# One product for three k chunks, weight sums moved, last products at fixed places and a second queue for the first loads, in a two-layer cross-attention kernel

## The chip, the cores and the metric

The kernel runs on one core of a Trainium2 chip. The metric is the device time of one execution in microseconds (us), launch to end. Several executions are timed and the median is given; one more execution is recorded by the hardware profiler, and all durations of single instructions come from that one.

## The reference

Two layers of cross-attention with a residual work on `x` (8 batches, 100 queries, 640 channels) and a context of 722 tokens of 1024 channels. The first 77 tokens are "text", the other 645 are "ip". Each layer has its own weights; all are f32. Shortened:

```python
q = split_heads(x @ Wq)                     # 20 heads of 32 channels
k, v       = text @ Wk, text @ Wv
k_ip, v_ip = ip @ Wk_ip, ip @ Wv_ip
out_text = softmax(q @ k.T * scale) @ v
# layer 0
out_ip = softmax(q @ k_ip.T * scale) @ v_ip
# layer 1: a shared term is added to the ip scores, and a mask is multiplied in
text_probs = softmax(q_all_heads @ k_all_heads.T * scale)
sem = (text_probs @ text) @ ip.T * scale
out_ip = (softmax(q @ k_ip.T * scale + 0.5 * sem) * mask) @ v_ip
x = (out_text + out_ip) @ Wo + bias + x
```

The context is the same in both layers, so the keys and values of both layers can be made without waiting for the attention.

## The kernel before

**Units and visits.** A unit `u` is one layer of one batch: 16 units, 0 to 7 for layer 0. Units go in `PAIRS` of two. The channels are cut into five chunks `c` of 128 (four heads). One step of the attention, called a visit here, is one pair (u, c) of the list `ORDER`: 80 visits, about 20 us each.

**The attention of a visit.** `scores` (L989) multiplies q by k into PSUM in two parts (512 and 210 columns). DVE takes maxima, ACT the exponentials (L1012, L1044), DVE the factors (L1034 to L1052). In the visit after, `transposes` (L1080) turn the probabilities by TensorE in six steps, through two PSUM tiles `pspt`; DVE or ACT copies each one out (L1087, L1085). Then `values` (L1103) multiplies by v into `pv`. `out_piece` (L901, `pso`) and `q_piece` apply the output weights and the next layer's q; the residual is added by DVE at L906. These small products take their PSUM from the same two tiles as `pspt`. `sem_text`, `sem_logits`, `sem_transpose` and `sem_scores` make the shared term of layer 1.

**Making k and v.** The 645 ip tokens of a pair are cut into five blocks of 128 (the last has 133). `pair_tasks` lists the products for the blocks (0, 1), (2, 3) and (4). Each matrix product is made of 2 x 2 halves by a scheme with seven products instead of eight: `seven` returns the seven steps in the order first, sixth, second, seventh, fifth, fourth, third. The steps use quarters of the weights (`b11` to `b22`) and sums of them (`t1` to `t4`, made by `weight_sums`, L134 to L137, in place where it can be), and in the same way sums of the tokens (`token_sums`, `third_sum`, `fourth_sum`). The sums for the pair that follows are made before it begins (`first_sums`). PSUM results `psv_*` and `psk_*` go through two banks; DVE and ACT move them to a tile of the pool `made` (two buffers), and GpSimd stores that to `k_d` and `v_d` in device memory. SP loads k and v back for each visit.

`v_steps` makes v (L613). `k_steps` makes the first four k chunks (L641). The fifth chunk of both layers is made together, only in layer 0's pairs, by `k4_steps` (L674) from weights of its own in `W4`, which lie in tiles that layer 1 uses later (`kt5`, `gt`, `g`, `sem`). For the block 4, `k_steps([0, 1])` multiplies matmuls of 133 columns, two chunks side by side (266 columns of a PSUM bank of 512), and `k4_steps` one chunk (133).

**The last pair.** Units 14 and 15 are made by `two_chunks` (L788, L793; v and k of two chunks in one product), and v of the fifth chunk by `fifth_chunk` (L828, `psv`, two halves for each of five blocks).

**What sets the order.** On TensorE, DVE and ACT the order is that of the code; on SP and GpSimd it is set by a scheduler of the framework. `production` gives every step a time in visits: `spread` puts a list of steps between two times so that each visit gets an even share, by the estimated cost of each step (the first number of a task; a cost of 0.0 marks work that is no product). `between` then puts the steps that are due into four slots of a visit: before the first transposes, between pairs of them, and before and after the last pair; from visit 74 on the third slot lies behind the last transposes. `apart` brings in the step that follows, when it is due within 0.4 visits (0.1 from visit 76 on), so that two parts of the attention don't stand side by side. `insert` puts extra tasks a number of steps ahead of a mark; `("k 4", 1, ...)` means ahead of the last step of block 4's k.

**The beginning.** The first lines of the work load, by SP alone, `xt` and `wq` in five row blocks each. The first product (`psq`, L279) needs one of each.

Of the kernel before, what the change touches and what calls it, by code (L numbers as in the profile page):

```python
# [44 lines left out]
def two_layer_xattn(  # L45
# [200 lines left out]
    with ExitStack() as es:  # L246
# [4 lines left out]
        )  # L251
        wq0 = []
        for k in range(NC_):
            nc.sync.dma_start(xt[:, :2, k], x_t[:, :2, k])
            t = fp.tile([P, C], F32, tag="wr", name=f"wq0_{k}", bufs=NCC)
            nc.sync.dma_start(t, wq[0][k * P : (k + 1) * P, :])
            wq0.append(t)
        for g in range(1, B // 2):
            nc.sync.dma_start(xt[:, 2 * g : 2 * g + 2], x_t[:, 2 * g : 2 * g + 2])
# [8 lines left out]
        nc.sync.dma_start(left_sb, left_t)  # L268
        nc.sync.dma_start(bias_sb, bias.rearrange("l p c -> p l c"))
        nc.sync.dma_start(mask_sb[:, 1:2], mask)  # L270


        for g in range(B // 2):
# [273 lines left out]
    def pair_tasks(us):  # L547
# [15 lines left out]
        for js in ((0, 1), (2, 3), (4,)):  # L563
# [68 lines left out]
            def k_steps(rs, js=js, n=n, operands=operands, pos=pos):  # L632

                made, ko = {}, {}
                m = n * len(js)

                def product(ps, which, go_on):
                    tokens = operands(which, None if len(js) == 2 else js[0])
                    for i, r in enumerate(rs):
                        for k in range(HK):  # L640
                            nc.tensor.matmul(  # L641
                                ps[:, i * m : (i + 1) * m],
                                lhsT=W["k", WHICH[which]][:, k, r * P : (r + 1) * P], rhs=tokens(k),
                                start=(i == 0 and k == 0 and not go_on), stop=(k == HK - 1), skip_group_check=True,
                            )

                def step(i):
                    if i == 0:
                        o = ko[0] = opool.tile([P, 2, 2, len(rs), m], F32, tag="made", name=f"ko_{us[0]}_{js[0]}_{rs[0]}")
                        made[0] = seven(  # L650
                            f"psk_{us[0]}_{js[0]}_{rs[0]}", product,
                            tuple(o[:, h, m].rearrange("p r n -> p (r n)") for h in range(2) for m in range(2)),
                        )
                    made[0][i]()
                    if i < 6:
                        return
                    for h, u in enumerate(us):
                        for j in js:
                            p0 = pos[j] * n
                            dst = k_d[u][:, :4, BLOCKS[j][0] : BLOCKS[j][1]].rearrange("p (m r) n -> p m r n", r=2)  # L660
                            for i, r in enumerate(rs):
                                nc.gpsimd.dma_start(dst[:, :, r], ko[0][:, h, :, i, p0 : p0 + n])  # L662

                return [(1.8, lambda i=i: step(i)) for i in range(7)]

            def k4_steps(js=js, n=n, operands=operands, pos=pos):

                made, ko = {}, {}
                m = n * len(js)

                def product(ps, which, go_on):
                    tokens = operands(which, None if len(js) == 2 else js[0])
                    for k in range(HK):
                        nc.tensor.matmul(  # L674
                            ps[:, :m], lhsT=W4[WHICH[which]][:, k, :], rhs=tokens(k),
                            start=(k == 0 and not go_on), stop=(k == HK - 1), skip_group_check=True,
                        )

                def step(i):
                    if i == 0:  # L680
                        o = ko[0] = opool.tile([P, 2, 2, m], F32, tag="made", name=f"k4_{us[0]}_{js[0]}")
                        made[0] = seven(
                            f"psk4_{us[0]}_{js[0]}", product, tuple(o[:, h, l2] for h in range(2) for l2 in range(2))
                        )
                    made[0][i]()
                    if i < 6:
                        return
                    for h, u in enumerate(us):
                        for l2 in range(2):
                            for j in js:  # L690
                                nc.gpsimd.dma_start(
                                    k_d[u + B * l2][:, 4, BLOCKS[j][0] : BLOCKS[j][1]],
                                    ko[0][:, h, l2, pos[j] * n : (pos[j] + 1) * n],
                                )

                return [(1.75 if len(js) == 2 else 0.95, lambda i=i: step(i)) for i in range(7)]

            def head(j, begin=begin):

                return [(0.0, lambda: begin(j))]  # L700
# [7 lines left out]
            first = us[0] == 0 and js[0] == 0  # L708
            if first:
                tasks.append((0.0, lambda: [load(j) for j in range(3)]))  # L710
            ks_ = k_steps([0]) + k_steps([1]) if len(js) == 2 else k_steps([0, 1])
            if first:

                v_load = (0.0, lambda: load_wv(wvi[0]))
                v_sums = (0.0, lambda: (weight_sums("v", HC, (nc.vector, nc.gpsimd)), load_text(us)))
                v = v_steps(0)
                tasks += head(0) + head(1) + [(0.0, load_w4), v_load] + with_sums(0, with_sums(1, ks_[:7]))
                tasks += [v_sums] + ks_[7:] + [(0.0, w4_sums)] + k4_steps()
                tasks += v[:2] + [(0.0, text_sum)] + v[2:] + v_steps(1)
            else:  # L720

# [4 lines left out]
                for j in js:  # L726
# [385 lines left out]
    def production():  # L1112
# [88 lines left out]
    def small_work(n):  # L1201
# [200 lines left out]
```

## Time and profile before

| | |
|---|---|
| median of 3 executions | 2058.15 us (2058.02 to 2060.34) |
| the profiled execution's own time | 2060.31 us |
| its span, first to last instruction | 2058.5 us |
| mean granted clock of TensorE | 0.999 |
| DMA, mean over the span | 123 GB/s |

The span is what the rows of the profile divide among the engines; the time of an execution also has a little around it. The profiled execution is one of the longer ones of these four. A row of instructions names the line, the engine, the operation, what is written and read, and the shapes. f32 matmuls show as two records each. PE is TensorE, PEld its weight loads, DVE is VectorE, ACT is ScalarE, POOL is GpSimd, SP issues loads. A few matmul records in a hundred can be missing.

The page in 40 slices of the span (tenths of busy time):

```text
PE   8999999999999999999999999999999999999998
DVE  2211222246555455554556665655665667788777
ACT  1001000033433333333333344444444545566666
```

The first fifth of the span has no attention yet: it makes the text's k and v and the first pair. The new layer's value products begin at about 1107 us, and the last ten visits take up the stretch from about 1917 us.

### The profile page before, as it was taken

How to read it: one execution, taken by the hardware profiler on the slowest of the kernel's cores; microseconds unless marked ns; L12 is line 12 of the kernel's file. 1: busy time of each engine (PE TensorE's matmuls, PEld its weight loads, DVE VectorE, ACT ScalarE, POOL GpSimd, SP SyncE). 2: the span in 40 equal slices, each digit the busy share in tenths (PEclk: the TensorE clock that was granted, in tenths of full speed). 3: DMA queues.
4: the chain of work that ended last, by engine and by line, in shares of the span. 5: the costliest groups of instructions: out<-in, count | busy, mean ns of one | idle time of the engine just before them, and what ended most of it. 6: DMA issues, size and time to landing. Idle time of an engine off the chain costs nothing. (4 is left out here: it accounts for less than half of the span.)

```text
span 2058.5 us, 38749 instructions
## 1 busy us (share of the span) xinstructions
PE 2028.2 (99%) x15154; PEld 1568.4 (76%) x15154; DVE 1118.0 (54%) x3053; ACT 785.0 (38%) x2255; POOL 310.2 (15%) x445
## 2 busy tenths in 40 slices
PE   8999999999999999999999999999999999999998
PEld 8676767776777867778677777777777778888876
DVE  2211222246555455554556665655665667788777
ACT  1001000033433343333333344444544445566666
POOL 3212312111111101111111001001010101111110
PEclk9999999999999999999999999999999999999999
DMA  9545223323432534326255354336342536545461
GB/s 330 155 131 170 88 75 92 98 76 93 115 94 74 155 96 107 85 89 171 71 146 141 102 156 121 84 99 179 100 117 79 152 95 168 165 125 151 120 180 54
DMA packets 296340, 252.20 MB, mean 123 GB/s; under 512 B 46622, under 2 KB 265170, under 8 KB 296158
## 3 DMA queue, kind: packets, MB, share of 16 engines
q1 hardware_dynamic: 274382, 181.29, 32.6%
q0 software_dynamic: 21776, 68.44, 9.4%
q8 instruction: 119, 1.95, 0.4%
q14 instruction: 63, 0.52, 0.1%
HBM read 180.74 MB, written 68.93 MB: 121 GB/s over the span
## 5 line engine op out<-in xcount | busy, mean ns | idle before, releaser
L1012 ACT ACTIVATE p<-sc,st 100x512 f32<-100x512 f32 (+1 forms) x320 | 165.5, 529 | 217.6 <-DVE st L998 135.4
L1087 DVE COPY pt<-pspt 128x400 f32<-128x400 f32 (+1 forms) x319 | 175.5, 568 | 102.5 <-PE pspt L1080 93.3
L1044 ACT ACTIVATE p<-p,st 100x512 f32<-100x512 f32 x320 | 207.6, 713 | 56.0 <-DVE st L1038 55.8
L1080 PEld LDWEIGHTS pspt<-ident,p 100*128 100x128 f32 (+1 forms) x1920 | 187.7, 137 | 44.3 <-DVE res L906 6.2
L1080 PE MATMUL pspt<-ident,p 100*128 100x100 f32 (+1 forms) x1920 | 211.9, 250 | 8.2 <-DVE res L906 3.8
L1012 ACT ACTIVATE p<-p,st 100x512 f32<-100x512 f32 (+1 forms) x320 | 176.7, 554 | 81.8 <-DVE st L1004 81.7
L1085 ACT COPY pt<-pspt 128x400 f32<-128x400 f32 x161 | 79.2, 492 | 287.5 <-PE pspt L1080 287.1
L613 PE MATMUL psv_a<-wv,x 128*128 128x397 f32 (+1 forms) x560 | 185.8, 474 | 0.4
L662 POOL DMA_DIRECT2D k_d<-ko x140 | 100.0, 718 | 506.1 <-DVE ko L223 455.1
L613 PE MATMUL psv_d<-wv,s 128*128 128x320 f32 (+1 forms) x560 | 174.3, 454 | 0.0
L613 PEld LDWEIGHTS psv_a<-wv,x 128*128 128x128 f32 x560 | 103.0, 189 | 68.8 <-issue 12.6
L1004 DVE CUSTOM_DVE_ANT_0 p<-sc,sem 100x512 f32<-100x512 f32 (+1 forms) x320 | 138.7, 490 | 21.7 <-PE sc L989 21.5
L613 PEld LDWEIGHTS psv_d<-wv,s 128*128 128x128 f32 x560 | 104.1, 190 | 54.8 <-issue 4.3
L998 DVE TENSOR_REDUCE st<-sc 100x2 f32<-100x1024 f32 (+1 forms) x160 | 125.2, 824 | 29.0 <-PE sc L989 29.0
L989 PE MATMUL sc<-k,q 32*100 32x210 f32 (+1 forms) x1280 | 138.5, 502 | 0.9 <-DMA k<-k_d 0.9
L641 PE MATMUL psk_d<-s,wk 128*128 128x256 f32 (+1 forms) x672 | 136.5, 348 | 0.0
L628 POOL DMA_DIRECT2D v_d<-vo x70 | 38.8, 555 | 647.2 <-DVE gst L603 327.2
L641 PE MATMUL psk_a<-x,wk 128*128 128x256 f32 (+1 forms) x672 | 135.7, 347 | 0.6 <-ACT ko L197 0.6
L641 PEld LDWEIGHTS psk_a<-x,wk 128*128 128x128 f32 x672 | 109.0, 189 | 21.4 <-issue 5.0
L641 PEld LDWEIGHTS psk_d<-s,wk 128*128 128x128 f32 x672 | 108.2, 189 | 18.5 <-issue 4.8
L613 PE MATMUL psv_e<-wvt,x 128*128 128x397 f32 (+1 forms) x280 | 92.6, 472 | 0.0
L1103 PEld LDWEIGHTS pv<-pt,v 128*32 128x32 f32 x3200 | 67.5, 110 | 26.8 <-issue 13.6
(225 smaller groups left out, 3325.0 us busy)
## 6 DMA issues: line engine op xcount, KB each, us to landing
x<-ip_t SPq DMA_DIRECT2D x80, 512.0 KB
k<-k_d SPq DMA_DIRECT2D x80, 322.5 KB
v<-v_d SPq DMA_DIRECT2D x80, 320.0 KB
v_d<-vo POOLq DMA_DIRECT2D x70, 320.0 KB, 2.7
k_d<-ko POOLq DMA_DIRECT2D x112, 128.0 KB, 4.8
o<-wo SPq DMA_DIRECT2D x35, 320.0 KB
x<-ip_t SPq DMA_DIRECT2D x20, 532.0 KB
q<-wq SPq DMA_DIRECT2D x20, 320.0 KB
```

What stands on the lines that cost most here:

```text
L613: nc.tensor.matmul(ps[:, :m], lhsT=tokens(k)[:, :P], rhs=w[:, k, :], start=(k == 0 and not go_on), stop=(k == HK - 1), skip_group_check=True,)
L641: nc.tensor.matmul(ps[:, i * m : (i + 1) * m], lhsT=W["k", WHICH[which]][:, k, r * P : (r + 1) * P], rhs=tokens(k), start=(i == 0 and k == ...
L662: nc.gpsimd.dma_start(dst[:, :, r], ko[0][:, h, :, i, p0 : p0 + n])
L989: nc.tensor.matmul(scs[i // 2][:S, i % 2, : k1 - k0], lhsT=qs_[u][rows, c, :], rhs=ks[u, c][rows, k0:k1], start=True, stop=True)
L998: nc.vector.tensor_reduce(st[:, part, 2 * h : 2 * h + 2], scs[h][:S, :, :n], AX.X, ALU.max, negate=True)
L1004: nc.vector.tensor_tensor_reduce(out=p[:, i, k0 : k0 + n], in0=scs[h][:S, i % 2, :n], in1=sems[u][:, k0 : k0 + n], scale=-1.0, scalar=3.0e ...
L1012: nc.scalar.activation(dst, dst if l else scs[h][:S, i % 2, :n], AF.Exp, bias=st[:, part, i : i + 1], scale=-1.0 if l else 1.0, accum_out= ...
L1044: nc.scalar.activation(p[:, i, :KA], p[:, i, :KA], AF.Copy, scale=mul[:, 0, i : i + 1])
L1080: nc.tensor.transpose(ps[:rows, i * S : (i + 1) * S], pr[u, c][:, i, j * P : j * P + rows], ident[:S, :S])
L1085: nc.scalar.copy(dst, src)
L1087: nc.vector.tensor_copy(dst, src)
L1103: nc.tensor.matmul(ps[32 * i : 32 * i + 32, :S], lhsT=lhs, rhs=pt[:rows, j, i * S : (i + 1) * S], start=(j == 0), stop=(j == 5),)
```

## The change

It has four parts.

1. `k_steps` takes the chunk index 2 for the fifth chunk, with the weights of `W4`; `k4_steps` is gone. For two blocks at a time the fifth chunk stays a set of products of its own, with an estimated cost of 1.8 in place of 1.75. For block 4 in layer 0 all three chunks are side by side in one set of seven products (399 columns), with an estimated cost of 2.7 where there were 0.95 and 1.8.
2. At the change of layers (pair 3), the first two of layer 1's v weight sums are inserted three and two steps ahead of the mark, where they were one and none ahead.
3. The last pair's `two_chunks` products are spread up to visit n + 3.1 instead of n + 3.4 (n is 70), and the ten halves of `fifth_chunk` get written-out times from n + 3.3 to n + 8.1. The second `sem_text` step of unit 15 moves from the second slot to the first.
4. The first `xt` block is issued by ACT's queue, the first `wq` block by SP in two pieces (256 and 384 columns). DVE clears a tile `zeros`, and TensorE multiplies it by itself four times, into a PSUM tile that nobody reads, ahead of the first product.

```diff
         for k in range(NC_):
-            nc.sync.dma_start(xt[:, :2, k], x_t[:, :2, k])
             t = fp.tile([P, C], F32, tag="wr", name=f"wq0_{k}", bufs=NCC)
-            nc.sync.dma_start(t, wq[0][k * P : (k + 1) * P, :])
+            rows = wq[0][k * P : (k + 1) * P, :]
+            if k == 0:
+                nc.scalar.dma_start(xt[:, :2, k], x_t[:, :2, k])
+                nc.sync.dma_start(t[:, : 2 * P], rows[:, : 2 * P])
+                nc.sync.dma_start(t[:, 2 * P :], rows[:, 2 * P :])
+            else:
+                nc.sync.dma_start(xt[:, :2, k], x_t[:, :2, k])
+                nc.sync.dma_start(t, rows)
             wq0.append(t)
...
+        zeros = fp.tile([P, 2 * S], F32, tag="zeros", name="zeros")
+        nc.vector.memset(zeros, 0.0)
+        ps = product_ps("zeros_ps")
+        for _ in range(4):
+            nc.tensor.matmul(ps[:, : 2 * S], lhsT=zeros[:, :P], rhs=zeros, start=True, stop=True)
...
                 def product(ps, which, go_on):
                     tokens = operands(which, None if len(js) == 2 else js[0])
+                    x = WHICH[which]
                     for i, r in enumerate(rs):
+                        w = W4[x] if r == 2 else W["k", x][:, :, r * P : (r + 1) * P]
                         for k in range(HK):
                             nc.tensor.matmul(
                                 ps[:, i * m : (i + 1) * m],
-                                lhsT=W["k", WHICH[which]][:, k, r * P : (r + 1) * P], rhs=tokens(k),
+                                lhsT=w[:, k, :], rhs=tokens(k),
...
                             for i, r in enumerate(rs):
-                                nc.gpsimd.dma_start(dst[:, :, r], ko[0][:, h, :, i, p0 : p0 + n])
+                                src = ko[0][:, h, :, i, pos[j] * n : (pos[j] + 1) * n]
+                                if r < 2:
+                                    nc.gpsimd.dma_start(dst[:, :, r], src)
+                                else:
+                                    for l2 in range(2):
+                                        nc.gpsimd.dma_start(k_d[u + B * l2][:, 4, cols], src[:, l2])
...
-            def k4_steps(js=js, n=n, operands=operands, pos=pos):
...
-                return [(1.75 if len(js) == 2 else 0.95, lambda i=i: step(i)) for i in range(7)]
+                t = 2.7 if len(rs) == 3 else 1.8
+                return [(t, lambda i=i: step(i)) for i in range(7)]
...
-            ks_ = k_steps([0]) + k_steps([1]) if len(js) == 2 else k_steps([0, 1])
+            if len(js) == 2:
+                ks_ = ([] if l else k_steps([2])) + k_steps([0]) + k_steps([1])
+            else:
+                ks_ = k_steps([0, 1] if l else [0, 1, 2])
...
-                tasks += ([] if l else k4_steps()) + ks_
+                tasks += ks_
...
-                ("k 4", 1, v[:1]),
-                ("k 4", 0, v[1:2] + [(0.0, lambda: load_quarters("k", wki[1], 2 * P))]),
+                ("k 4", 3, v[:1]),
+                ("k 4", 2, v[1:2]),
+                ("k 4", 0, [(0.0, lambda: load_quarters("k", wki[1], 2 * P))]),
...
-        for a, b, tasks in (
-            (n - 10 - AHEAD, n + 3.4, lists[: 2 * NB]),
-            (n + 3.4, n + 8.95, lists[2 * NB :]),
-        ):
-            plan.append((a, b, [t for one_list in tasks for t in one_list]))
-        return [task for a, b, tasks in plan for task in spread(a, b, tasks)]
+        plan.append((n - 10 - AHEAD, n + 3.1, [t for one_list in lists[: 2 * NB] for t in one_list]))
+        placed = [task for a, b, tasks in plan for task in spread(a, b, tasks)]
+        at = [n + 3.3] + [n + p + x for p in range(4, 8) for x in (0.1, 0.7)] + [n + 8.1]
+        for t, f in [t for one_list in lists[2 * NB :] for t in one_list]:
+            placed.append((t, at.pop(0) if t else at[0], f))
+        return placed
...
-            at[1].append((0.4, lambda: sem_text(z, 1)))
+            at[0].append((0.4, lambda: sem_text(z, 1)))
```

More of the change, by code (lines that the diff above doesn't have):

```diff
@@ L638, in product @@
                     tokens = operands(which, None if len(js) == 2 else js[0])
+                    x = WHICH[which]
                     for i, r in enumerate(rs):
+                        w = W4[x] if r == 2 else W["k", x][:, :, r * P : (r + 1) * P]
                         for k in range(HK):
                             nc.tensor.matmul(
-                                ps[:, i * m : (i + 1) * m],
-                                lhsT=W["k", WHICH[which]][:, k, r * P : (r + 1) * P], rhs=tokens(k),
+                                ps[:, i * m : (i + 1) * m], lhsT=w[:, k, :], rhs=tokens(k),
                                 start=(i == 0 and k == 0 and not go_on), stop=(k == HK - 1), skip_group_check=True,
@@ L648, in step @@
                     if i == 0:
-                        o = ko[0] = opool.tile([P, 2, 2, len(rs), m], F32, tag="made", name=f"ko_{us[0]}_{js[0]}_{rs[0]}")
+                        o = ko[0] = opool.tile(
+                            [P, 2, 2, len(rs), m], F32, tag="made", name=f"ko_{us[0]}_{js[0]}_{rs[0]}"
+                        )
                         made[0] = seven(
@@ L658, in step @@
                         for j in js:
-                            p0 = pos[j] * n
-                            dst = k_d[u][:, :4, BLOCKS[j][0] : BLOCKS[j][1]].rearrange("p (m r) n -> p m r n", r=2)
+                            cols = slice(BLOCKS[j][0], BLOCKS[j][1])
+                            dst = k_d[u][:, :4, cols].rearrange("p (m r) n -> p m r n", r=2)
                             for i, r in enumerate(rs):
-                                nc.gpsimd.dma_start(dst[:, :, r], ko[0][:, h, :, i, p0 : p0 + n])
@@ L664, in k_steps @@
-                return [(1.8, lambda i=i: step(i)) for i in range(7)]
-            def k4_steps(js=js, n=n, operands=operands, pos=pos):
[L668 to L694, printed above, removed]
-                return [(1.75 if len(js) == 2 else 0.95, lambda i=i: step(i)) for i in range(7)]
@@ L716, in pair_tasks @@
                 v = v_steps(0)
+                ks_ = ks_[7:] + [(0.0, w4_sums)] + ks_[:7]
                 tasks += head(0) + head(1) + [(0.0, load_w4), v_load] + with_sums(0, with_sums(1, ks_[:7]))
-                tasks += [v_sums] + ks_[7:] + [(0.0, w4_sums)] + k4_steps()
+                tasks += [v_sums] + ks_[7:]
                 tasks += v[:2] + [(0.0, text_sum)] + v[2:] + v_steps(1)
```

## The prediction

> **What bounds the kernel now.** I began with the busy time of the engines, the first part of the page.
>
> ```profile
> span 2058.5 us, 38749 instructions
> PE 2028.2 (99%) x15154; PEld 1568.4 (76%) x15154; DVE 1118.0 (54%) x3053; ACT 785.0 (38%) x2255; POOL 310.2 (15%) x445
> ```
>
> TensorE works 2028.2 of 2058.5 us, so new orders and fewer waits can win 30.3 us at most. Which of it does the change reach? TensorE's own waits say where it lies. The columns: who waited, for whom, us in total, times, longest us.
>
> ```profile
> PE psq L279 <- DMA wq<-wq: 5.3, 1, 5.3
> PE pspt L1080 <- DVE res L906: 3.8, 13, 1.1
> PE psv_b L613 <- DVE wvt L135: 2.9, 1, 2.9
> PE pv L1103 <- DVE pt L1087: 2.4, 3, 0.8
> PE psk_d L674 <- DVE k L217: 1.3, 2, 0.6
> ...
> PE psk_c L674 <- DVE k L202: 0.8, 2, 0.4
> ...
> PE psk_d L674 <- DVE k L212: 0.4, 1, 0.4
> ...
> PE psk_b L674 <- PE psk_a L674: 0.2, 1, 0.2
> ```
>
> Four places, and the change touches each: the first load (5.3); the separate product of the fifth k chunk, L674 (1.3 + 0.8 + 0.4 + 0.2 = 2.7); one wait of `psv_b` for a weight sum (2.9); and the end, where `pspt` waits for the residual's addition and `pv` for a copy.
>
> The 2.9 costs more than it shows. A table by stage around it (stretch, length, busy us of PE, PEld, DVE, ACT, POOL with counts, granted clock, DMA share, GB/s), then TensorE in order of time:
>
> ```profile
> 1109.00:1110.00 1.00, 0.00 (x0) 0.00 (x0) 1.00 (x3) 1.00 (x2) 0.00 (x0) 1.00 1.12 413
> ...
> 1112.00:1113.00 1.00, 1.00 (x2) 0.67 (x3) 0.71 (x2) 0.00 (x0) 0.00 (x0) 0.50 0.56 165
> ...
> 1115.00:1116.00 1.00, 1.00 (x22) 0.56 (x24) 0.22 (x1) 0.00 (x0) 0.00 (x0) 1.00 0.40 152
> ```
>
> ```profile
> 1106.65 2.34 PE L613 MATMUL psv_a<-wv,x 128*128 128x320 f32 x8
> 1111.86 3.82 PE L613 MATMUL psv_b<-wvt,s 128*128 128x320 f32 x8 [2.86 <-DVE wvt L135]
> ```
>
> After the pause the clock stands at 0.50 and eight matmuls like those before take 3.82 instead of 2.34 us: 1.5 more, 4.4 in all. The beginning shows the same. The clock column reads 1.00 there, but between 6 and 8 us four matmul records start per us, between 9 and 11 eight: half pace from 5.27 to about 8.8.
>
> The end, TensorE in order of time:
>
> ```profile
> 2001.27 0.74 PE L1080 MATMUL pspt<-ident,p 100*128 100x100 f32 x4
> 2003.13 0.56 PE L1080 MATMUL pspt<-ident,p 100*128 100x100 f32 x4 [1.13 <-DVE res L906]
> ...
> 2007.82 1.07 PE L1103 MATMUL pv<-pt,v 128*32 128x100 f32 x40 [0.24 <-ACT pt L1085]
> 2009.70 0.38 PE L1103 MATMUL pv<-pt,vt 82*32 82x100 f32 x8 [0.81 <-DVE pt L1087]
> ```
>
> A visit with no product ahead of `pso` waits 0.7 to 1.1 at `pspt`; one with no product behind the last transposes waits 0.24 + 0.81 at `pv`.
>
> **What the Trainium skill says.** "TensorE: Matmul & The Clock Gate", Part 1 (The HAM clock gate): the array runs at half rate until it was busy through a window of about 3.4 us, the window is free-running, and an idle window brings half rate back. The trace agrees: 0.50 from about 1111.3 to 1114.7 us, and 3.5 us of half pace at the start. It doesn't say how full a window must be, and that is open for the new warm-up. "DMA: Bandwidth & Descriptors", section "Issuing engines are not separate DMA queues": a second issuing queue saves only the sequencer's time. The trace has that time: each first issue takes SP 0.43 to 0.47 us.
>
> **The change part by part.**
>
> *First loads and four products of zeros.* Before, the first product needs `xt` (100 KB, issued at 0.74) and a whole `wq` row block (320 KB, issued at 1.24), and starts at 5.27. Traffic begins at about 1.8 us; by the GB/s slices 420 KB have moved at about 3.8, so completion adds some 1.4. After, ACT issues `xt` while SP issues the first 128 KB of `wq`, both at about 0.74: 228 KB at the 200 to 300 GB/s of these slices are there at 2.7 to 3.0, plus 1.4 gives 4.1 to 4.4. Start earlier by 0.9 to 1.2; I take 1.0. The other 192 KB come 0.5 us later, behind four half-pace matmul records of 0.25 us. On ACT the table load (1.28 us) stands behind this issue; its first evict is at 14.74, so nothing waits. Later blocks arrive every 420 KB / 330 GB/s = 1.3 us and are used up in ten records of 0.174 = 1.7, so the lead isn't lost to loads; nor does TensorE wait for a DMA again before 1975 us. The four products (eight records, 2.0 us at half pace) fall into idle time, from about 1.3 to 3.3. If they fill a window, the following fourteen slow records take 0.125 less each: 1.75. If not, nothing. I take 0.8. Together -1.8 (0 to -3.0).
>
> *The fifth chunk in the block-4 product.* Per layer-0 pair, 7 x 8 matmuls of 133 columns and 7 x 4 of the same width become 7 x 12: no matmul less. The 14 evictions become 7 (266 and 133 columns: 0.43 and 0.29 us on DVE; 399 columns: about 0.57). A product then lasts 24 records instead of 16 or 8. Sixteen take 1.82 us, so 2.73, and DVE has that long to empty a bank; at 8 records (0.9 us) it was late, at 16 (L641) never; there TensorE waited only once, 0.6 us, for ACT. So the 2.7 us of L674 go; I take -2.6 (-1.5 to -2.8). GpSimd issues the same eight stores of about 0.7 us, but all at the end of the product: the fifth chunk's four come up to 4 x 0.7 = 2.8 us behind the others. They are read a visit (20 us) or more later. If that cover were gone, `sc` would wait at most those 2.8 us per pair.
>
> *Weight sums sooner.* The subtraction into `t3` (L134, 1.48) moves from before the last product to before the last three, that into `t2` (L135, 1.48) ahead of two products. Worked out from the order: the value products end at 1080.2, seven products of 2.73 with the attention's work between end at about 1104.6; `t3` runs at about 1095, `t2`, behind the next pair's token sums (2 x 0.69), at about 1100 to 1101.5, and `psv_b` wants it at about 1107.8. So it is 6 us early, its 2.86 go, and with them the half clock. DVE's eviction of the fifth product stands behind `t2` and comes about 1 us late; its bank is asked for at 1105.5. The last quarter that `t3` needs was issued by SP at 1080.21, 15 us ahead. On SP the loads of wk go ahead of five `kt` loads, which the code uses some nine visits later. -4.4 (-2.9 to -4.6, the small end for an execution whose window doesn't fall in the pause).
>
> *Last products.* In the visits that begin at 1975, 1987, 1998, 2010 and 2021 the waits on DVE and ACT add up to 1.8, 0.3, 2.2, 0.3 and 1.4. By the changed order every one of the first four has a product behind its last transposes, and all but the third have one ahead of `pso`: 0.3, 0.3, 1.2, 0.3, 1.4. That is 6.0 - 3.5 = 2.5. The visit before them gets its four transposes in a row, some 0.3. `sc` waits 0.9 for `k_d` at 1976; in the new order its last store is issued earlier by one piece of a visit, but about as much of TensorE's work leaves from between, so I count nothing (0.9 lost or won). Moving a `psm` step to the first slot keeps its pauses (0.3 to 0.8 each) but one, about 0.3. I take -2.1 (0 to -3.5): DVE is busy 47 of 58 us here and may give part back.
>
> *New places of the other products.* Costs of 1.8 for 1.75 shift layer 0's tasks past transposes and scores. No wait of TensorE on attention stands in that stretch, so this can only cost: 0 (0 to +1.5).
>
> Sum: 1.8 + 2.6 + 4.4 + 2.1 = 10.9. The profiled execution took 2060.31 (span 2058.5 and 1.8 around it), which gives 2049.4. It is 2.2 above the median of the three runs, 2058.15; if those have no half clock at the pause, they win 1.5 less: 2058.15 - 9.4 = 2048.75. I say 2049.0.
>
> **The rivals.** *The leads don't last*: the windows don't count the warm-up and the sum only changes whom `psv_b` waits for. For: DMA is busy 98% of the first 60 us. Against: no DMA wait follows there. Left are 2.6 + 2.1, less 1.5 for shifts: 2058.15 - 3.2 = 2055.0. *The end doesn't move*: DVE's chain sets it; 2051.1. *Slower*: in the merged stretches of pairs 1 to 3, two visits each, evictions of 0.57, token sums and `t3` stand on DVE ahead of the softmax's factors, the transposes wait for these, and the clock halves as at 1111. Six such stretches at 4.4 are 26.4: 2049 + 26.4 = 2075. It decides from 3 stretches on (13 us). Against: value products of like length (2.7 us) run beside the same softmax without a wait. *The edit is not what it says*: a merged product with other matmuls would show in their count; the order shows the same number and eight more records.
>
> **How the numbers follow.** Forecast 0.66, the end unmoved 0.16, leads lost 0.13 (a quarter of it still under 2054), slower 0.05. A measurement of this kernel can tell about 0.2%, 4.1 us: faster means under 2054.0. The forecast's own ends, 2058.15 less the small ends of the terms (4.4) and 2060.31 less the large ones (13.9), are 2053.75 and 2046.4; with a median run losing all, 2045.5. The range 2045.5 to 2054.5 takes in these and the unmoved end. Faster 0.85, same 0.10, slower 0.05.
>
> **What would show it.** Right: `psq` starts at 4.1 to 4.4; L674 has no line of waits and the merged product none on DVE; no `psv_b` wait for L135 and no half clock near 1105; one visit with a `pv` pause after 1970 us, not three. Wrong: a new `pspt` or `sc` wait between 440 and 1100 us, or a DVE wait for a `wv` load at L134.

## The result, and the profile after

| | before | after |
|---|---|---|
| median of 7 executions | 2058.14 us (2057.33 to 2060.34) | 2051.88 us (2048.74 to 2053.84) |
| ratio to before, 95% interval | | 0.9967 [0.9955, 0.9978] |
| the profiled execution's own time | 2060.31 us | 2051.88 us |
| its span | 2058.5 us | 2050.1 us |

The change makes the kernel 6.3 us faster, where 9.1 were forecast: 2051.88 for 2049.0, inside the range of 2045.5 to 2054.5. The total hides more than that. One term was larger than forecast, one came to nothing, and one was lost again between 50 and 160 us after it was won. The busy time of the engines:

```profile
span 2050.1 us, 38709 instructions
PE 2029.3 (99%) x15162; PEld 1572.1 (77%) x15162; DVE 1115.3 (54%) x3034; ACT 783.3 (38%) x2247; POOL 310.3 (15%) x445
```

TensorE works as long as before (2029.3 for 2028.2, the zeros included), so all that is won is waiting time. TensorE's waits:

```profile
PE pspt L1075 <- DVE res L901: 3.2, 13, 1.1
PE pspt L1075 <- DVE pt L1082: 1.7, 7, 0.4
PE pv L1098 <- DVE pt L1082: 1.5, 2, 0.8
PE pskt_d L334 <- issue: 1.3, 1, 1.3
PE zeros_ps L284 <- DVE zeros L281: 1.2, 1, 1.2
PE pv L1098 <- ACT pt L1080: 1.0, 2, 0.8
PE pspt L1075 <- ACT sem L879: 1.0, 2, 0.8
```

The waits of the fifth chunk's product and of `psv_b` are gone, and the zeros have a line of their own. The second line (0.5 before), the waits for ACT and one with no releaser, `pskt_d <- issue`, have grown. The last was in before as well, in a line that the prediction did not show:

```profile
PE pskt_d L320 <- issue: 1.0, 1, 1.0
```

At the layer change, TensorE of after in order of time:

```profile
1101.28 2.34 PE L627 MATMUL psv_a<-wv,x 128*128 128x320 f32 x8
1103.46 2.31 PE L627 MATMUL psv_b<-wvt,s 128*128 128x320 f32 x8
```

`psv_b` follows at once and at full pace: 2.31 us where it was 3.82 after a wait of 2.86. The start:

```profile
1.17 3.03 PE L284 MATMUL zeros_ps<-zeros 128*128 128x200 f32 x8 [1.17 <-DVE zeros L281]
```

`psq` starts at 3.99; its records start 0.33 us apart until 5.99 and 0.17 apart from there. In before they start 0.33 apart from 5.73 to 8.73. (The counts in a table by stage take in every record that touches a stretch. The prediction read them as starts: its four per us were three, and its 0.25 us for a record at half pace is 0.33.) The end, in the visit whose `pso` stands alone, and the table by stage of two of its microseconds:

```profile
1989.86 1.96 PE L896 MATMUL pso<-hs,o 128*128 128x200 f32 x10
1991.66 0.74 PE L1075 MATMUL pspt<-ident,p 100*128 100x100 f32 x4
1993.52 1.05 PE L1075 MATMUL pspt<-ident,p 100*128 100x100 f32 x8 [1.13 <-DVE res L901]
1994.76 0.56 PE L1075 MATMUL pspt<-ident,p 100*128 100x100 f32 x4 [0.19 <-DVE pt L1082]
...
1997.08 3.06 PE L823 MATMUL psv<-wv,x 128*128 128x128 f32 x16
```

```profile
1997.00:1998.00 1.00, 1.00 (x7) 1.00 (x6) 0.93 (x5) 1.00 (x6) 0.00 (x0) 0.50 0.82 220
1998.00:1999.00 1.00, 1.00 (x6) 1.00 (x6) 0.72 (x4) 1.00 (x6) 0.00 (x0) 0.50 0.41 132
```

Behind the pause of 1.13 us stands a half clock that was not in before: `psv` takes 3.06 us for its usual 1.97.

**A ledger of leads.** The same landmarks of TensorE in each profile, as the lead over before in us, show where time is won and lost. The landmarks, with their time in before: ACT's first q eviction (14.74), the first `psvtr` of layer 0 (79.59), the first `psvt_a` of layer 1 (171.46), the first visit's scores (407.2), the scores behind the layer change (1128.0), the last visit's second scores (2039.6), the end of the span (2058.5). The kernels below "after" are the experiments'; "again" is after itself, once more. Each lead is rounded to 0.1.

| | q | psvtr | psvt_a | first scores | layer change | last scores | end |
|---|---|---|---|---|---|---|---|
| after | 2.1 | 1.8 | 1.1 | 1.1 | 9.9 | 8.8 | 8.4 |
| again | 2.1 | 1.3 | -0.3 | -0.3 | 8.5 | 9.0 | 8.7 |
| old_sums | 1.9 | 1.4 | 0.6 | 0.6 | 9.3 | 8.2 | 7.8 |
| no_merge | 1.9 | 1.1 | 0.3 | 0.4 | 3.7 | 4.2 | 3.7 |
| old_end | 1.5 | 2.4 | 1.4 | 1.4 | 10.2 | 10.8 | 10.4 |
| no_start | 0.5 | 0.2 | 0.2 | 0.2 | 8.7 | 9.2 | 9.1 |
| no_zeros | 1.2 | 2.5 | 2.5 | 2.5 | 11.3 | 10.1 | 9.8 |
| best | 0.7 | 0.1 | 0.1 | 0.1 | 8.9 | 9.4 | 9.0 |

From the first scores to the layer change every kernel with the merged product gains the same 8.8 us (8.7 in old_sums, 8.5 in no_start). What differs from profile to profile lies ahead of the first scores and in the last 300 us. Single executions of a kernel lie some 5 us apart, so parts of 1 to 2 us are told by these landmarks, hardly by the medians.

### The profile page after: what moved, and what is told of

The parts are those of the page before. It is cut to its first block, busy times and chain, and to the rows that moved or that the text cites. A ratio compares the mean times of both kernels' runs of the same rounds, so it can differ in the third digit from the quotient of the medians.

```text
span 2050.1 us, 38709 instructions
## 1 busy us (share of the span) xinstructions
PE 2029.3 (99%) x15162; PEld 1572.1 (77%) x15162; DVE 1115.3 (54%) x3034; ACT 783.3 (38%) x2247; POOL 310.3 (15%) x445
## 4 chain that ended last, share of the span: by engine, by line
PE 96%; DVE 3%; ACT 1%; issue 0%; ACTq 0%; DVEq 0%
PE psv_a L627 9%; PE psv_d L627 8%; PE psk_a L657 8%; PE pspt L1075 8%; PE psk_d L657 8%; PE sc L984 6%; PE pv L1098 4%; PE psv_e L627 4%; PE psk_c L657 4%; PE psk_b L657 4%; PE psv_c L627 4%; PE psv_b L627 4%; PE psk_e L657 4%; PE pso L896 3%; PE psq L293 2%; PE psq L915 2%
```

## The experiments

Each kernel ran in five rounds beside before. The medians of before were 2060.38 (again, old_end, near3, old_sums), 2060.42 (with the second four) and 2058.38 (the last four); so the ratios are compared.

**After once more, and which edit brings the layer change.** The prediction gave the end of the `psv_b` wait to the sums. Its rival: the merged product alone already gives DVE the time.

`again`: no edit.

> The changed kernel once more, as the measure for the three others of this group. Both theories: 2051.9 us in the median, ratio to before about 0.997, single executions spread over some 5 us, because the half-clock windows fall at other places in each.

Measured: 2052.04 us (2049.36 to 2053.57), ratio 0.9960 [0.9948, 0.9972], the time of after. The ratio is lower than the 0.9967 above, and the gain 8.3 us and not 6.3, because the median of before is 2.2 us higher here: its executions lie partly near 2058 and partly above 2060. What decides between the two was not traced.

`old_sums`:

```diff
-                ("k 4", 3, v[:1]),
-                ("k 4", 2, v[1:2]),
-                ("k 4", 0, [(0.0, lambda: load_quarters("k", wki[1], 2 * P))]),
+                ("k 4", 1, v[:1]),
+                ("k 4", 0, v[1:2] + [(0.0, lambda: load_quarters("k", wki[1], 2 * P))]),
```

> The changed kernel with the two weight sums at their old distance from the mark (one and none ahead). Theory A: psv_b waits again for about 2.5 to 3 us and, when the window falls in the pause, eight matmuls run at half clock: 3 to 4.5 us slower, about 2055 to 2056. Rival (the longer product of block 4 alone gave DVE the time): no wait above 1 us, within 1 us of the changed kernel.

Measured: 2051.8 us (2048.9 to 2054.05), ratio 0.9958 [0.9946, 0.9970], the same as after. TensorE at the layer change, with the sums back at their old places:

```profile
1101.76 2.34 PE L627 MATMUL psv_a<-wv,x 128*128 128x320 f32 x8
1103.98 2.39 PE L627 MATMUL psv_b<-wvt,s 128*128 128x320 f32 x8
```

No wait at `psv_b`. DVE's second sum in old_sums:

```profile
1102.36 1.48 DVE L135 TENSOR_TENSOR wvt<-wvt,wv 128x1280 f32<-128x1280 f32 x1
```

It ends at 1103.84, 0.14 us ahead of `psv_b`. In after it ends at 1097.44, 6.0 us ahead, just as the prediction worked out. So with the merged product in, moving the sums brings room and no time: the rival is right, by a narrow margin.

`no_merge`, the sums staying moved:

```diff
-                t = 2.7 if len(rs) == 3 else 1.8
+                t = 2.7 if len(rs) == 3 else 0.95 if rs == [2] and len(js) == 1 else 1.8
...
-                ks_ = k_steps([0, 1] if l else [0, 1, 2])
+                ks_ = k_steps([0, 1]) if l else k_steps([2]) + k_steps([0, 1])
```

> Block 4's fifth k chunk is a product of its own again (8 matmul records), all else as after, the sums at their sooner places. If the merged product is what took the four waits at the k product and also the wait of psv_b, both come back: 2.7 us at the k product, up to 2.9 at psv_b with half a clock window behind it (1.5): 4 to 7 us slower than after, a ratio to before of 0.998 to 1.000. If either edit alone keeps psv_b from waiting, only the 2.7 come back: a ratio of about 0.9975, and no wait of psv_b. If the merged product brought nothing at all, 0.9963 as after.

Measured: 2056.42 us (2054.16 to 2059.61, 18 runs), ratio 0.9982 [0.9975, 0.9989]: 0.0022 above again, 4.4 us by the medians. The lines of TensorE's waits that after doesn't have or has smaller:

```profile
PE psk_d L657 <- DVE ko L217: 1.3, 2, 0.6
PE psk_c L657 <- DVE ko L202: 1.1, 3, 0.4
...
PE psv_a L627 <- DVE ko L223: 0.8, 1, 0.8
...
PE psk_d L657 <- DVE ko L212: 0.4, 1, 0.4
```

The fifth chunk's waits come back; that of `psv_b` doesn't, though `psv_a` just ahead of it waits 0.8. Before, old_sums, no_merge and after are the four combinations of the two edits, the start and the end lie outside this stretch, and their gain from the first scores to the layer change is 0, 8.7, 3.3 and 8.8 us. Each edit alone ends the `psv_b` wait; the second adds nothing to the first. The merged product alone brings it all.

**The last products.** Theory A: what the fixed places win they lose at visit 76. `apart` brings steps ahead by up to 0.4 visits, so visit 73 gets two halves of the fifth chunk and visit 76 only one, and its `pso` stands alone. Theory B: the fixed places win what the prediction said, and the missing part is lost elsewhere.

`old_end`: the two `spread` lists and the place of `sem_text` as before, all else as after.

> The changed kernel with the last products spread as before (to visit n + 3.4, then to n + 8.95) and the second sem_text step back in its slot. Theory A (the fixed places win about 2 us of waits and give it back as a stretch at half clock in visit 76 and as pauses in visit 73): within 1 us of the changed kernel; in the profile a sc wait on k_d of about 0.9 us is back, and three pv pauses. Theory B (as predicted, the fixed places win 2.1): 2 us slower than the changed kernel, about 2054.

Measured: 2049.83 us (2048.92 to 2051.62), ratio 0.9952 [0.9940, 0.9964]: by the medians 2.2 us faster than again, which neither theory had. The three `pv` pauses are back, and `sc` waits 0.3 for `k_d`. From the layer change to the last scores it gains 0.6 us on before, and that is this one wait: before has 0.9 there, old_end 0.3, and all other listed waits of the last 300 us are alike. (`best` and `best_x` below, with the same end, wait 0.4 and not at all, and gain 0.5 and 0.8.) With the new end there are two cases: again gains 0.5, and after loses 1.1. TensorE in old_end, in the visit that answers to the one above:

```profile
1988.65 1.96 PE L896 MATMUL pso<-hs,o 128*128 128x200 f32 x10
1990.44 0.74 PE L1075 MATMUL pspt<-ident,p 100*128 100x100 f32 x4
1992.31 0.56 PE L1075 MATMUL pspt<-ident,p 100*128 100x100 f32 x4 [1.13 <-DVE res L901]
1992.71 1.97 PE L823 MATMUL psv<-wv,x 128*128 128x128 f32 x16
```

The same pause of 1.13 us, but a full product follows it at once. In after short transposes follow, with further gaps. In those windows after and old_sums and no_zeros, three of eight profiles with this end, have a half clock (1.7 us); the profiles of before, old_end and of the two versions below that keep the old end have none there. That the transposes behind the pause tip the window is read from this; no run shows it by itself. The executions that were only timed agree that the new end meets a half clock more often: the mean clock of after's profiled execution is 0.998 and that of again's 0.999, and 0.998 stands in 12 of the 38 executions of the seven kernels with exactly this end and the merged product, and in none of the 15 with the old one (old_end, `best`, `best_x`).

TensorE's waits of the last 300 us (from 1745 us on in before, 1736 in after) say why the new end gains little even without a half clock. Won: `pv` for DVE 2.4 to 1.5, `pspt` for the residual 2.9 to 2.3, `pspt` for `tpt` 1.1 to 0.8, `sc` for `k_d` 0.9 to 0. Lost: `pspt` for DVE's copies 0.5 to 1.7, `pspt` for `sem` 0.5 to 1.0, `pv` for ACT 0.7 to 1.0. That is 2.7 won and 2.0 lost. Of the waits for DVE's copies, 0.9 at `pspt` and 0.7 at `pv` lie ahead of 1975 us, and so do 0.8 for ACT at `pv`, where before has none of the three, and 1.0 for `sem`, where before has 0.5: in the visits that get the same `two_chunks` products within less time and the first halves of the fifth chunk behind them.

`near3`:

```diff
-            near = 0.4 if n < NC_ * LAST[0] + 6 else 0.1
+            near = 0.4 if n < NC_ * LAST[0] + 3 else 0.1
```

> The changed kernel, but steps are pulled in up to 0.4 visits ahead only before visit 73, so that visits 74 to 77 each have one product ahead of pso and one behind the last transposes, and visit 73 has one instead of two. Theory A: the pause of 1.13 and the half clock of visit 76 (1.6) go, visit 73 gets a pv pause of about 1 and perhaps 0.5 at sc: 1 to 2 us faster than the changed kernel, about 2050. Theory B (DVE's chain sets the pace of these visits): no difference within 0.5.

Measured: 2052.11 us (2050.51 to 2053.16), ratio 0.9960 [0.9949, 0.9972]. The pause of 1.13 is gone, and nothing is won: `sc` waits 0.98 for `k_d` at 1966 us, and behind it, together with the `pv` pauses of 0.24 and 0.81, the profile has a half clock from 1966.7 to 1970.1. So visit 76 isn't the cause that theory A made of it: with that pause gone, others are in its place.

`end_34`:

```diff
-        plan.append((n - 10 - AHEAD, n + 3.1, [t for one_list in lists[: 2 * NB] for t in one_list]))
+        plan.append((n - 10 - AHEAD, n + 3.4, [t for one_list in lists[: 2 * NB] for t in one_list]))
...
-        at = [n + 3.3] + [n + p + x for p in range(4, 8) for x in (0.1, 0.7)] + [n + 8.1]
+        at = [n + 3.45] + [n + p + x for p in range(4, 8) for x in (0.1, 0.7)] + [n + 8.1]
```

> As after, with the products of the first four k chunks spread to n + 3.4 instead of n + 3.1 (n is the first visit of the last element but one), as before; the fifth chunk's halves stay at their fixed places, with the first at n + 3.45. The kernel with all of the old end was about 2 us faster than after. If what costs is the denser work ahead of n + 3.1, this one is as fast as that: a ratio of about 0.9952. If the fixed places themselves cost it, it stays at after's 0.9960 or slower.

Measured: 2053.64 us (2051.2 to 2054.84), ratio 0.9968 [0.9956, 0.9980]. `pspt` waits 0.9 for DVE's copies instead of 1.7, so half of the denser work's price is gone; but `sc` waits 1.8 for `k_d` in one piece, the pause of 1.13 stays, and its profile has the half clock behind it. So the denser work isn't all of it: the fixed places cost as well. `sem_text`'s move was not tried alone; it is in this kernel too, and `pspt` waits 0.5 for `sem` here as in before, so the 1.0 of after came with the denser work.

**The start.** The prediction had the lead last, since TensorE waits for no DMA later.

`no_start`: first loads as before and no zeros, all else as after.

> The first loads as before and no products of zeros, all else as after. By the traces the start put TensorE 2.1 us ahead at the first q eviction, and no wait for a load follows: if that lead lasts to the end, 2.1 us slower than after, a ratio of about 0.9975, with psq at 5.2 to 5.3 us and full pace from about 8.8. If the lead doesn't last (rival), the same as after, 0.9963.

Measured: 2051.68 us (2050.34 to 2052.63), ratio 0.9960 [0.9947, 0.9972], the same as again. `psq` starts at 4.56 here with the loads of before, so that start itself moves by 0.7 between executions. The ledger has the reason: of 2.1 us at the q eviction, again has 1.3 left at `psvtr` and nothing at `psvt_a`. The first loss is the `issue` wait of `pskt_d`. DVE, then TensorE, of again in order of time:

```profile
53.53 0.69 DVE L236 TENSOR_TENSOR s<-x 128x512 f32<-128x512 f32 x1 [1.52 <-DMA x<-ip_t]
54.26 0.69 DVE L237 TENSOR_TENSOR s<-s,x 128x512 f32<-128x512 f32 x1
58.81 0.69 DVE L236 TENSOR_TENSOR s<-x 128x512 f32<-128x512 f32 x1 [3.86 <-DMA x<-ip_t]
59.42 0.47 DVE L212 TENSOR_TENSOR kt<-pskt_c,kt 128x308 f32<-128x308 f32 x1
...
61.00 0.47 DVE L217 TENSOR_TENSOR kt<-pskt_d,kt 128x308 f32<-128x308 f32 x1
```

```profile
61.58 2.31 PE L334 MATMUL pskt_d<-s_text,wk 128*128 128x308 f32 x8 [1.87 <-issue]
```

The token sum L236 stands ahead of the evictions in DVE's order and waits 3.86 us for an x load; `pskt_c` and `pskt_d` are emptied late, and the next `pskt_d` starts 0.11 us after that eviction ends (61.00 + 0.47). The same distance of 0.10 lies between the two in before (62.27 + 0.47, then 62.84), in after and in no_start, though the order of these sums and evictions on DVE is not the same in every kernel. So the landing of x sets the pace here, whatever the start did. The Trainium skill, "PSUM — Partial Sum Buffer", section "Engine vs sequencer instructions", has the rule behind it, that the vector engine's queue is strict FIFO; the trace agrees.

`no_zeros`: the five lines of the zeros taken out, the loads staying new.

> After without the four products of zeros: the first loads are still the new ones. If the zeros count for the clock, psq starts at about 4.0 us as in after, but goes at half pace to about 7.3 instead of 6.0, and the first q eviction comes 0.6 to 1.0 us later than in after (12.62). If they count for nothing, the half pace ends where it does in after, near 6.0. The time can hardly tell 0.8 us; the trace does.

Measured: 2050.06 us (2049.04 to 2051.27), ratio 0.9952 [0.9940, 0.9965]. `psq` starts at 3.54, goes at half pace to about 8, and the first q eviction comes at 13.50 instead of 12.62. This pair alone doesn't show that the zeros count for the clock: the half pace ends where a clock window ends (see the last section), and without zeros that is at 8.0 here, at 9.3 in `best` and at 6.5 in `best_x`, with first q evictions at 13.50, 14.03 and 12.66; in the kernels with the four zeros these lie at 12.62 to 13.24. The profile of near3 does show it:

```profile
1.17 3.00 PE L284 MATMUL zeros_ps<-zeros 128*128 128x200 f32 x8 [1.17 <-DVE zeros L281]
3.99 1.86 PE L293 MATMUL psq<-xt,wq 128*128 128x200 f32 x10
6.59 32.38 PE L293 MATMUL psq<-xt,wq 128*128 128x200 f32 x190 [0.73 <-DMA wq<-wq]
```

Its `psq` goes at full pace from the first record, when TensorE had done nothing but zeros. Even so its first q eviction comes at 12.62, as in after, where full pace began two microseconds later: `psq` waits 0.73 for a `wq` block, so that here the loads set the pace. In the mean the eviction comes 0.6 us sooner with the four zeros than in the three kernels with the new loads alone. They also stand in the way: the loads are in at 3.3 to 3.5 us (3.54 here, 3.44 and 3.32 in the two last kernels), and `psq` has to wait for the zeros until 3.99.

And they cost something later, where nobody would look. TensorE in the last text product of layer 1, again:

```profile
161.45 3.44 PE L356 MATMUL psvtr<-wv,text 128*52 128x320 f32 x23
165.94 5.86 PE L356 MATMUL psvtr<-wv,text 128*52 128x320 f32 x41 [1.05 <-issue]
171.73 2.42 PE L375 MATMUL psvt_a<-wv,text 128*128 128x320 f32 x8
```

and no_zeros:

```profile
160.22 8.83 PE L351 MATMUL psvtr<-wv,text 128*52 128x320 f32 x64
168.98 2.42 PE L370 MATMUL psvt_a<-wv,text 128*128 128x320 f32 x8
```

From the start of `psvtr` to `psvt_a` it takes 10.28 us for 8.76. All eight profiles with the four zeros take 0.6 to 1.5 us longer than that here; seven show the break after 23 of the 64 records, in one (end_34) it is too short to be listed. All five without zeros take 8.75 or 8.76.

`zeros8`:

```diff
-        for _ in range(4):
-            nc.tensor.matmul(ps[:, : 2 * S], lhsT=zeros[:, :P], rhs=zeros, start=True, stop=True)
+        for _ in range(8):
+            nc.tensor.matmul(ps[:, :S], lhsT=zeros[:, :P], rhs=zeros[:, :S], start=True, stop=True)
```

> After with eight products of zeros of 100 columns instead of four of 200: the same time on TensorE, but sixteen records more ahead of everything else, not eight. Seven kernels with the four products pause after 23 of the 64 records of psvtr near 165 us; three without don't. If the pause sits at a fixed count of TensorE's instructions, it moves eight records ahead, to after 15 of psvtr, and grows by what eight records take, about 1.1 us, to 1.3 to 2.1. If it belongs to the data or to the product, it stays after 23 at 0.2 to 1.1.

Measured: 2051.43 us (2048.95 to 2053.34), ratio 0.9964 [0.9952, 0.9977]. TensorE in the same product:

```profile
159.18 2.36 PE L356 MATMUL psvtr<-wv,text 128*52 128x320 f32 x15
162.05 6.94 PE L356 MATMUL psvtr<-wv,text 128*52 128x320 f32 x49 [0.51 <-issue]
168.93 2.42 PE L375 MATMUL psvt_a<-wv,text 128*128 128x320 f32 x8
```

The break moves eight records ahead, to behind the 15th, as for a fixed count of TensorE's instructions: in all nine profiles with zeros it comes behind TensorE's 855th matmul record, and in the five without nothing happens there. Its cost doesn't grow: 9.75 us to `psvt_a`, 1.0 more than without, where 1.3 to 2.1 were expected. The place was right, the size wrong. What happens at that count is open: just ahead stand 128 very short matmuls (`psgl`), and the profile has two transfers of its instruction queue between 160 and 170 us, but in kernels without the break as well.

`wk4_act`:

```diff
-        load_wk4(src)
+        load_wk4(src, nc.sync if src is wkt[0] else nc.scalar)
 
-    def load_wk4(src):
+    def load_wk4(src, queue=nc.sync):
...
-        nc.sync.dma_start(W["k", 4], src.rearrange("(k p) n -> p k n", p=P)[:, :, 4 * P :])
+        queue.dma_start(W["k", 4], src.rearrange("(k p) n -> p k n", p=P)[:, :, 4 * P :])
```

> After with one load moved from SP's queue to ACT's: the text product's fifth weight chunk of layer 1, which waits for a tile that TensorE reads until 47 us and holds the first x loads behind it on SP. If the start's lead is lost there (DVE stands in a token sum that waits for x, and the eviction of pskt_c and pskt_d behind it), the x loads land some 4 us sooner, TensorE's pause of 1.3 to 1.9 us at the second pskt_d near 61 us goes, and psvtr starts at 76.5 us instead of 77.8 to 78.3: 1.3 to 1.9 us faster than after. If the pause has another cause, or the DMA is so full that x lands no sooner, it stays.

Measured: 2050.03 us (2049.76 to 2053.99), ratio 0.9961 [0.9948, 0.9973]. The wait and its releaser:

```profile
PE pskt_d L334 <- issue: 0.3, 1, 0.3
```

```profile
51.26 1.39 DVE L236 TENSOR_TENSOR s<-x 128x512 f32<-128x512 f32 x1 [4.43 <-DMA x<-ip_t]
...
56.68 0.69 DVE L236 TENSOR_TENSOR s<-x 128x512 f32<-128x512 f32 x1 [3.04 <-DMA x<-ip_t]
```

The first x blocks are there 2.3 us sooner than in again, the second 2.1, where 4 were expected; TensorE waits 0.3 instead of 1.9, and `psvtr` starts at 76.93 (again: 78.34). In no_zeros and zeros8 the second x block is there at 57.64 and 56.42 without this edit, and they have no such wait either, zeros8 with the same order on DVE as again; so the wait goes with the landing, as the theory has it. How much of the earlier landing is this edit's and how much chance, one profile doesn't tell. In the median nothing of it can be told, as for all parts of this size.

**A version that keeps what held.** `best` is after without the zeros and with the old end; `best_x` has the load on ACT's queue as well.

> The version that the runs point to: after without the products of zeros and with the old end. In the traces the old end is worth 0.1 us over the new one, 1.7 more where a half-clock window falls into the pause of the new one, and leaving out the zeros 0.6 to 1.5 at psvtr less 0.9 at the start. If these add up: 2047.5 to 2049.5 us, a ratio to before of 0.9940 to 0.9950. If the kernels so far differ only by chance, 2051 to 2052 as after.

> The same, with the load of layer 1's fifth text weight chunk on ACT's queue. No wait at the second pskt_d in any execution: the same as the version without it where that has no such wait, up to 1.9 us faster where it has; 2047 to 2049 us.

Measured: `best` 2048.66 us (2048.13 to 2051.69), ratio 0.9953 [0.9939, 0.9966]; `best_x` 2049.09 us (2048.37 to 2049.77), ratio 0.9952 [0.9939, 0.9964]. The times are about those expected, the ratios just above them. `best` still waits 1.6 us at `pskt_d` in its profile, `best_x` 0.4, where none was expected; the span of `best_x` is 2046.6, the shortest of all. The three kernels with the old end lie at 0.9952 and 0.9953; the nine with the new one or one near it and the merged product (after and its repeat among them) at 0.9952 to 0.9968, 0.9961 in the mean. That is 0.0009, some 1.8 us; the profiles account for a part of it only, the half clock's 1.7 us in about one execution of three. Each interval by itself overlaps after's, so better than after is likely for `best` and not shown for it alone; against before both are 9.3 to 9.7 us faster.

## Why the prediction was right, and where not

**Fifth chunk in the block-4 product, and weight sums: near in sum, wrong in which edit.** 2.6 + 4.4 = 7.0 were forecast for the two, 8.8 came. By the scores at 1062 us, 2.7 were won, and 6.1 more at the layer change, there the 2.86 and the half clock's 1.5 with them. Less these 4.4, which came as forecast, 4.4 are left for the fifth chunk, where 2.6 stood. Two things failed. The step "so it is 6 us early, its 2.86 go" put these 4.4 to the sums' new places, but the working counted with the merged products' length already in it (seven of 2.73 us). Costed one at a time, the merged product would have been seen to suffice, since it puts 0.9 us more of TensorE's work into each step that DVE has. And the 2.7 of L674 were too small, because the list leaves out waits of 0.15 us or less, and counts a wait only from the modelled end of the matmul before. In before:

```profile
581.39 1.08 PE L674 MATMUL psk_a<-x,w_a 128*128 128x133 f32 x8
582.48 1.17 PE L674 MATMUL psk_b<-s,w 128*128 128x133 f32 x8
```

From start to start that is 1.09 us for eight records that follow each other in 0.91 when nothing holds them, and no wait is listed. Over the block-4 products of pairs 1 to 3 these distances add up to 5.1 us more than 0.91 each, twice the 2.5 that are listed there.

**First loads and zeros: the forecast at the place was right (1.8, and 2.1 came at the first q eviction), the lead didn't last.** The failing step is "so the lead isn't lost to loads; nor does TensorE wait for a DMA again before 1975 us". It looked at TensorE's waits for DMA only. DVE waited for one, and TensorE for DVE; in the list that was the 1.0 us `issue` line of before. In the eight profiles with the new loads and the four zeros the lead at the first scores is -0.3 to 1.6, 0.8 in the mean, and no_start's time equals after's. *The leads don't last* was right for this term, though not because the windows leave the warm-up out; nearer was its other argument, that DMA is busy 98% of the first 60 us. In detail: the loads came at 3.3 to 3.5, not at 4.1 to 4.4, and the zeros lasted to 4.2, not 3.3, since a record took 0.38 us, not 0.25. The open question of the warm-up has its answer from near3: the windows count it.

**Last products: wrong.** 2.1 were forecast, and the doubt stood beside it ("DVE is busy 47 of 58 us here and may give part back"). The runs show a gain of 0.5 or a loss of 1.1 to 1.2 on before, and the old end beside the other edits gains 0.6. In the five visits themselves the reading held: their waits fell from 6.0 to 3.8 us in after, where 3.5 were read. The step that failed read the changed order for pauses at `pv` and `pso` only, with the visits from 1975 on, and counted nothing for the 14 visits ahead that became denser, where the lost waits lie. *The end doesn't move* is the nearest rival (2051.1, measured 2051.88).

**New places of the other products: right at 0.** Between 440 and 1100 us after has one wait of TensorE, 0.3 us at `psv_a`, no wait of DVE for a `wv` load, and no half clock in the merged stretches; the *slower* rival has nothing for it.

**The sum.** From before's profile to after's, 1.1 + 8.8 - 1.1 and 0.4 less at the very end make the 8.4 of the spans. Forecast were 1.8 + 7.0 + 2.1 = 10.9. The total came near by luck in part: the larger gain at the layer change paid for some of what the start and the end didn't bring.

## What to carry to other kernels

Follow a lead along a row of landmarks to the end, since what is won at the start is lost at the next place where something else sets the pace; a small `issue` wait of the busy engine is such a place, and the queue of the engine that empties its banks shows the reason. Where two edits may end the same wait, cost each alone. A list of waits leaves out the shortest: where a product is too short for its evictions, compare the distance of its starts with that of undisturbed ones.

## What the runs showed of the hardware

- **A window of 3.4 us can count as idle with two thirds of it busy.** In after the half clock begins at 1995.96 and ends at 1999.36, 3.4 us later. These times are worked out from the clock in the two stretches at its edges, 0.98 and 0.82:

```profile
1995.00:1996.00 1.00, 1.00 (x14) 0.60 (x13) 0.64 (x2) 0.23 (x1) 0.00 (x0) 0.98 0.29 102
...
1999.00:2000.00 1.00, 1.00 (x9) 0.95 (x7) 0.73 (x4) 0.16 (x1) 0.00 (x0) 0.82 0.00 0
```

In the 3.4 us ahead of it TensorE idles 1.0 of the 1.13, and 0.19: 1.2 us. The Trainium skill, "TensorE: Matmul & The Clock Gate", Part 1, has an idle window bring half rate back and doesn't say how idle. Part 4 (PE-mode transpose) states that transposes don't count as busy in the same way; 1.6 of the 2.2 us that ran in this window are transposes.
- **Idle time alone doesn't decide it.** Within each of the fourteen profiles the clock changes lie whole multiples of 3.41 us apart (in after at 5.98, 1995.95 and 1999.37: 583 and 1), so a profile tells where its windows lay. Near 60 us windows of no_start, `best` and near3 idle 1.3, 1.6 and 1.7 us beside full products, with no transpose in them, and the clock stays full. After's window idles less and loses it, which fits the transposes. It is a near thing: again's window from 1992.55 to 1995.96 has the same 1.2 us idle and 1.6 of transposes, with 0.6 of `pso` where after has 0.6 of `sc`, and keeps the clock.
- **Eight records more at the front moved a break at 165 us.** TensorE paused behind its 855th matmul record, for 0.6 to 1.5 us in all, in each of the eight profiles with four products of zeros, and behind the same one with eight (`zeros8`); in the five without it did not.
- **The middle is exact.** From the first scores to 1752 us, 1345 us of work, after and its repeat show the same gain on before at every landmark, to 0.1 us; all of their spread lies in the first 407 us, where the loads' landings vary, and in whether a clock window falls into a pause near the end.
